# Routed experts computed on tokens sorted by expert, in two groups of batches

## The chip, the cores and the metric

The kernel runs on one core of a Trainium2 chip. Its time is the device time of the whole execution, in microseconds (us). A profiled execution records every instruction of the core's engines: TensorE (PE, with its weight loads as PEld), VectorE (DVE), ScalarE (ACT), GpSimd (POOL) and the issuing queue of SyncE (SP). Its span runs from the first to the last recorded instruction; the execution is a little longer than its span.

## The reference

The input x has 8 batches of 512 tokens with 256 features. A gated cross-attention (16 heads of 64, 512 context rows of 128 features) is added to x, and then a gated mixture of experts: 8 experts, of which each token uses the two with the largest router probability.

```python
x = x + tanh(g_xattn) * xattn(layernorm(x), ctx)      # 16 heads, softmax over 512 rows

xt = layernorm(x)                                     # 4096 tokens x 256
probs = softmax(xt @ gate_w.T)                        # 8 experts
routing_weights, selected = top_k(probs, 2)
comb = sum(one_hot(selected, 8) * routing_weights)    # zero but for two experts a token
for e in range(8):
    out = out + (xt @ expert_w[e].T + expert_b[e]) * comb[:, e:e+1]
x = x + tanh(g_ffn) * out
```

All of it is float32. The reference multiplies every token by every expert and lets the zeros of `comb` remove six of eight.

## The kernel before

A batch is 16 steps (`NS`), and the eight batches follow one another without a gap. A step handles two units; a unit is 128 query tokens of one pair of heads. Each step s does this, in program order:

1. `scores` of its two units on TensorE and `softmax` (the row maximum L230 on DVE, two exponentials L234 on ACT for each unit);
2. side work that is put early: `load_batch` and `experts`;
3. for the units of the step before, the 32x32 transposes on DVE (L255) and, in every even step, `exchange`: 16 transfers of 128 KB between partitions, issued by SP (L266), which finish the transposition of the probabilities; and for its own units the normalisation on POOL (L245);
4. the rest of the side work: projections (`proj_q`, `proj_k`, `proj_v`), attention times values (`values`, three steps after the exchange), `out_proj`, LayerNorm, router and so on.

There is no planner that weighs costs. The list built by `at(b, r, fn)` says in which step (16 b + r) a piece of side work stands, and the list `rank` says in which order the pieces of one step are emitted. Every engine works through its own part of that order and never overtakes. Buffers come from rotating pools (four PSUM banks called `ps_m` for all side work, two of double size, `ps_s`, for the scores).

The expert layer of batch b lies in the steps 22 to 51 after the batch's start, so it runs under the attention of the next two batches. `ln_stats`, `ln_rstd`, `ln_apply` and `ln_T` make the normalised, transposed tokens; `logits` (L318) and `route1` to `route3` give the gate of each token and expert, in `cg`. `weights_T` and `expert_bias` add the bias. Then 16 calls of `experts`, one a step, multiply 128 tokens by two experts each (L403) and DVE adds the two results to the token rows, each scaled by its gate (L410). All eight experts are done for all tokens. Their weights, 2 MB, stay in `we_sb` from the start. After the last expert of a tile SP writes it out (L414).

The last scores are in step 127. The steps after it finish batch 7 and the dense experts that are left.

Of the kernel before, what the change touches and what calls it, by code (L numbers as in the profile page):

```python
# [9 lines left out]
F32 = mybir.dt.float32  # L10
AF = mybir.ActivationFunctionType
ALU = mybir.AluOpType
AX = mybir.AxisListType

P = 128
LN_EPS = 1e-5


@with_exitstack
def kernel(  # L20
# [29 lines left out]
    const = ctx.enter_context(tc.tile_pool(name="const", bufs=1))  # L50
    xpool = ctx.enter_context(tc.tile_pool(name="xpool", bufs=4))
    work = ctx.enter_context(tc.tile_pool(name="work", bufs=2))
    single = ctx.enter_context(tc.tile_pool(name="single", bufs=1))
    qkp = ctx.enter_context(tc.tile_pool(name="qkp", bufs=2))
    vp = ctx.enter_context(tc.tile_pool(name="vp", bufs=2))
    aop = ctx.enter_context(tc.tile_pool(name="aop", bufs=NP_))
    ppool = ctx.enter_context(tc.tile_pool(name="ppool", bufs=4))
    ptp = ctx.enter_context(tc.tile_pool(name="ptp", bufs=2))
    xTp = ctx.enter_context(tc.tile_pool(name="xTp", bufs=2))
    route = ctx.enter_context(tc.tile_pool(name="route", bufs=2))  # L60
    small = ctx.enter_context(tc.tile_pool(name="small", bufs=4))
# [27 lines left out]
    nc.scalar.dma_start(out=gts[:, 1:2], in_=g_ffn.partition_broadcast(P))  # L89
    bo_bc = const.tile([P, D], F32, name="bo_bc")  # L90
    nc.scalar.dma_start(out=bo_bc, in_=bo.partition_broadcast(P))
    wo_sb = const.tile([P, NP_, D], F32, name="wo_sb")
    gw_sb = const.tile([P, KD, E], F32, name="gw_sb")
    we_sb = const.tile([P, KD, E * O], F32, name="we_sb")

# [3 lines left out]
    rev = const.tile([P, NT, E], F32, name="rev")  # L99
    cgs = [const.tile([P, NT, 32], F32, name=f"cg_{i}") for i in range(2)]  # L100

    ident = const.tile([P, P], F32, name="ident")
# [4 lines left out]
    def late_setup():  # L107

        nc.sync.dma_start(out=wo_sb, in_=wo.rearrange("(c p) d -> p c d", p=P))
        nc.sync.dma_start(out=gw_sb, in_=gate_wT.rearrange("(k p) e -> p k e", p=P))  # L110
        nc.sync.dma_start(out=we_sb, in_=expert_wT.rearrange("(k p) f -> p k f", p=P))
        nc.gpsimd.memset(eb2, 0.0)
        for t in range(NT):
            nc.sync.dma_start(out=eb2[32 * t : 32 * t + E, ts(t % 2, O)], in_=expert_b)
        nc.scalar.activation(tg, gts, AF.Tanh)

        nc.gpsimd.tensor_scalar(tgbo, bo_bc, tg[:, 0:1], 1.0, ALU.mult, ALU.mult)

        for e in range(E):
            nc.gpsimd.memset(rev[:, :, e : e + 1], float(E - e))  # L120

        for cg in cgs:
            nc.gpsimd.memset(cg, 0.0)

    def gate_wo(c):
# [21 lines left out]
    def ln_rstd(b, which):  # L147
        mv = lns[which, b][1]
        ve = small.tile([P, NT], F32, tag="ve", name=f"ve_{which}_{b}")
        nc.vector.tensor_scalar_add(ve, mv[:, :, 1], LN_EPS)  # L150
        rstd = small.tile([P, NT], F32, tag="rstd", name=f"rstd_{which}_{b}")
        nc.gpsimd.tensor_tensor(rstd, ve, mhalf, ALU.pow)
        xn = single.tile([P, NT, D], F32, tag="xn", name=f"xn_{which}_{b}")
        lns[which, b] += [rstd, xn]
# [8 lines left out]
    def ln_T(b, which):  # L163
        xn = lns.pop((which, b))[3]
        xT = xTp.tile([P, KD, N], F32, tag=which, name=f"xT_{which}_{b}")
        xTs[which, b] = xT
        for k in range(KD):
            tp = ps_m.tile([P, NT, P], F32, tag="m", name=f"lnT_{which}_{b}_{k}")
            for t in range(NT):
                nc.tensor.transpose(tp[:, t, :], xn[:, t, ts(k, P)], ident)  # L170
            nc.scalar.copy(xT[:, k, :], tp.rearrange("p t n -> p (t n)"))
# [137 lines left out]

    def te(tag, b, w=E):  # L310
        return route.tile([P, NT, w] if w > 1 else [P, NT], F32, tag=tag, name=f"{tag}_{b}")

# [30 lines left out]
    def route2(b):  # L343
        d1, ex, mk1 = rt[b]

        d2 = te("d2", b)
        nc.vector.scalar_tensor_tensor(d2, mk1, -3.0e38, d1, ALU.mult, ALU.add)
        m2 = te("m2", b, 1)
        nc.vector.tensor_reduce(m2, d2, AX.X, ALU.max)
        eq2 = te("eq2", b)  # L350
        nc.vector.tensor_tensor(eq2, d2, bc(m2), ALU.is_equal)
        key2 = te("key2", b)
        nc.vector.tensor_tensor(key2, eq2, rev, ALU.mult)
        km2 = te("km2", b, 1)
        nc.vector.tensor_reduce(km2, key2, AX.X, ALU.max)
        mk2 = te("mk2", b)
        nc.vector.tensor_tensor(mk2, key2, bc(km2), ALU.is_equal)
        mk = te("mk", b)
        nc.vector.tensor_tensor(mk, mk1, mk2, ALU.add)
        rt[b] = (ex, mk)  # L360

    def route3(b):

        ex, mk = rt[b]
        se = te("se", b, 1)
# [8 lines left out]
        )  # L374
        rt[b] = cg

    def weights_T(b):

        pc = ps_m.tile([P, 512], F32, tag="m", name=f"pc_{b}")[:, :P]
        nc.tensor.transpose(pc, rt[b].rearrange("p t e -> p (t e)"), ident)  # L380
        cgT = work.tile([P, P], F32, tag="cgT", name=f"cgT_{b}")
        nc.scalar.copy(cgT, pc)
        xTs["c", b] = cgT

    def expert_bias(b):
# [7 lines left out]
        for h in range(2):  # L393
            nc.vector.tensor_tensor(
                xs[b][:, 2 * h : 2 * h + 2, :], pbs[h], xs[b][:, 2 * h : 2 * h + 2, :], ALU.add
            )

    def experts(b, t, e2):

        xT, acc, cg = xTs["f", b], xs[b][:, t, :], rt[b]  # L400
        pe = ps_m.tile([P, 2, O], F32, tag="m", name=f"pe_{b}_{t}_{e2}")
# [22 lines left out]

    rank = [load_batch, experts, proj_k, proj_q, expert_bias, proj_v, weights_T, out_proj]
    rank += [ln_T, logits, values, ln_stats, ln_rstd, ln_apply, add_bias, gate_wo]
    rank += [route1, route2, route3]

    for b in range(B):
        if b > 0:  # L430
# [4 lines left out]
            for t in range(NT):  # L435
                at(b, -7, ln_apply, b, "q", t)
            at(b, -6, ln_T, b, "q")
            at(b, -5, add_bias, b)
            at(b, -2, proj_q, b, 0)
# [8 lines left out]
        for hp in range(NP_):  # L448
            at(b, 2 * hp + 5, values, b, hp)
        for half in range(2):  # L450
            for t in range(NT):
                at(b, 13 + 8 * half + 2 * t, out_proj, b, half, t)
        for t in range(NT):
            at(b, 22 + 2 * t, ln_stats, b, "f", t)
        at(b, 28, ln_rstd, b, "f")
        for t in range(NT):
            at(b, 29, ln_apply, b, "f", t)
        at(b, 30, ln_T, b, "f")
        at(b, 31, logits, b)
        at(b, 32, route1, b)  # L460
        at(b, 33, route2, b)
        at(b, 34, route3, b)
        at(b, 35, weights_T, b)
        at(b, 36, expert_bias, b)
        for i in range(NT * E // 2):
            at(b, 36 + i, experts, b, i // (E // 2), i % (E // 2))
    for c in range(NP_ // 2):
# [20 lines left out]
    for s in range(max(plan) + 1):  # L488
# [4 lines left out]
        for fn, args in side:  # L493
            if fn in (load_batch, experts):
                fn(*args)
# [8 lines left out]
        for fn, args in side:  # L504
            if fn not in (load_batch, experts):
                fn(*args)
# [37 lines left out]
```

## Time and profile before

| | |
|---|---|
| median of 3 runs | 1126.23 us (1124.82 to 1130.35) |
| the profiled execution | 1126.08 us |
| its span | 1124.2 us |
| TensorE busy | 1098.1 us, 98% of the span |
| VectorE busy | 865.1 us, 77% |
| ScalarE busy | 516.3 us, 46% |
| GpSimd busy | 384.2 us, 34% |
| HBM read and written | 11.71 MB and 4.19 MB |

A page of the profile gives the busy time of each engine, the busy share of 40 slices of the span in tenths, the chain of work that ended last, and the costliest groups of instructions with their mean duration. The trace behind it can be asked for single stretches of time, for the order of an engine's instructions, and for waits. Matrix products appear as two instructions each[...]: the `x8` of a step's scores are four products.

### The profile page before, as it was taken

The numbers are of one execution on the slowest core, as the hardware profiler recorded it, in microseconds if no ns is written. First come the engines' busy times: TensorE is split into PE (matmuls) and PEld (weight loads), VectorE is DVE, ScalarE is ACT, GpSimd is POOL, SyncE is SP. The second block draws the span as 40 slices with busy tenths as digits, with TensorE's granted clock in tenths as the row PEclk, the third lists the DMA queues.
The fourth block names the chain that finished last, engine by engine and source line by source line (L and its number), as shares of the span: only waits on it lengthen the run. The fifth ranks groups of instructions, "written<-read, shape, count | busy, mean of one in ns | idle before, by whom it ended". The sixth has DMA issues, their size and how long they took to land.

```text
span 1124.2 us, 13833 instructions
## 1 busy us (share of the span) xinstructions
PE 1098.1 (98%) x4008; PEld 496.2 (44%) x4008; DVE 865.1 (77%) x1448; ACT 516.3 (46%) x1330; POOL 384.2 (34%) x559
## 2 busy tenths in 40 slices
PE   6889999999999999999999999999999999999898
PEld 3334444544444444444445444444444444445443
DVE  4797788787887878878878778779787787786365
ACT  4666566554544444544444445445445445443000
POOL 4545335433343224323333323432334232331000
PEclk9999999999999999999999999999999999999899
DMA  6877786667555566556565475565665564565100
GB/s 221 191 163 167 172 189 150 150 150 171 122 120 133 127 157 143 113 129 139 138 141 128 107 172 133 113 150 113 146 154 118 118 145 111 129 152 132 35 15 19
DMA packets 61880, 151.05 MB, mean 134 GB/s; under 512 B 17872, under 2 KB 27248, under 8 KB 61552
## 3 DMA queue, kind: packets, MB, share of 16 engines
q1 hardware_dynamic: 60816, 148.75, 57.6%
q10 hardware_dynamic: 992, 1.44, 0.3%
q8 instruction: 33, 0.54, 0.2%
q14 instruction: 39, 0.32, 0.1%
HBM read 11.71 MB, written 4.19 MB: 14 GB/s over the span
## 4 chain that ended last, share of the span: by engine, by line
PE 91%; DVE 3%; SPq 3%; DMA 1%; issue 1%; ACT 0%; ACTq 0%; DVEq 0%
PE pe L403 20%; PE sc L220 20%; PE av L280 19%; PE po L298 10%; PE pq L199 9%; PE pk L209 5%; PE pv L189 5%; SPq L266 3%; PE pl L318 1%; DVE nm L230 1%; DVE tt L255 1%; PE pb L389 1%; PE lnT_f L170 1%; PE lnT_q L170 1%; DMA pt<-tt 0%
## 5 line engine op out<-in xcount | busy, mean ns | idle before, releaser
L245 POOL TENSOR_SCALAR p<-p,rs 128x512 f32<-128x512 f32 x512 | 345.0, 693 | 627.1 <-DVE rs L243 627.1
L234 ACT ACTIVATE p<-sc,nm 128x512 f32<-128x512 f32 x512 | 344.7, 685 | 234.6 <-DVE nm L230 230.4
L230 DVE TENSOR_REDUCE nm<-sc 128x2 f32<-128x1024 f32 x256 | 300.9, 1216 | 155.0 <-PE sc L220 155.0
L255 DVE STREAM_TRANSPOSE tt<-p 128x1024 f32<-128x1024 f32 x256 | 310.4, 1229 | 0.5 <-DMA pt<-tt 0.3
L220 PE MATMUL sc<-k,q 64*128 64x512 f32 x1024 | 256.6, 619 | 7.6 <-ACT p L234 7.6
L403 PE MATMUL pe<-we_sb,xT_f 128*128 128x512 f32 x512 | 246.9, 612 | 0.0
L280 PE MATMUL av<-pt,v 128*64 128x512 f32 x1024 | 236.6, 604 | 4.9 <-DMA out<-x 3.6
L410 DVE SCALAR_TENSOR_TENSOR x<-pe,cg,x 128x256 f32<-128x256 f32 x256 | 123.8, 484 | 75.8 <-PE pe L403 71.0
L403 PEld LDWEIGHTS pe<-we_sb,xT_f 128*128 128x128 f32 x512 | 89.1, 189 | 146.7 <-issue 115.7
L220 PEld LDWEIGHTS sc<-k,q 64*128 64x128 f32 x1024 | 88.3, 187 | 140.7 <-issue 108.3
L286 ACT COPY ao<-av 128x512 f32<-128x512 f32 x64 | 37.5, 586 | 228.9 <-PE av L280 228.9
L280 PEld LDWEIGHTS av<-pt,v 128*64 128x64 f32 x1024 | 68.6, 138 | 137.3 <-issue 128.0
L298 PE MATMUL po<-wo_sb,ao 128*128 128x256 f32 x512 | 122.1, 381 | 0.0
L199 PE MATMUL pq<-xT_q,wq_sb 128*128 128x512 f32 x256 | 121.3, 596 | 0.0
L298 PEld LDWEIGHTS po<-wo_sb,ao 128*128 128x128 f32 x512 | 95.9, 190 | 41.7 <-issue 29.3
L234 ACT ACTIVATION_READ_ACCUMULATOR p<-sc,nm 128x1 f32 x512 | 103.7, 203 | 0.0
L199 PEld LDWEIGHTS pq<-xT_q,wq_sb 128*128 128x128 f32 x256 | 48.9, 192 | 61.5 <-issue 59.3
L209 PE MATMUL pk<-ctxT,wk_sb 128*128 128x512 f32 x128 | 68.3, 615 | 6.8 <-DMA wk_sb<-in_wk 6.8
L189 PE MATMUL pv<-wv_sb,ctxT 128*128 128x256 f32 x256 | 66.2, 381 | 0.0
L189 PEld LDWEIGHTS pv<-wv_sb,ctxT 128*128 128x128 f32 x256 | 48.1, 190 | 35.2 <-issue 18.9
L203 ACT ACTIVATE q<-pq 128x512 f32<-128x512 f32 x64 | 38.8, 606 | 36.3 <-PE pq L199 36.3
L193 ACT COPY v<-pv 128x512 f32<-128x512 f32 x64 | 37.9, 593 | 20.1 <-PE pv L189 20.1
(61 smaller groups left out, 386.4 us busy)
## 6 DMA issues: line engine op xcount, KB each, us to landing
pt<-tt SPq DMA_DIRECT2D x1024, 128.0 KB, 2.4
out<-x SPq DMA_DIRECT2D x32, 128.0 KB, 2.1
x<-in_x SPq DMA_DIRECT2D x7, 512.0 KB, 3.8
ctxT<-in_ctxT SPq DMA_DIRECT2D x8, 256.0 KB, 2.9
we_sb<-in_expert_wT SPq DMA_DIRECT2D x1, 2048.0 KB, 12.8
wo_sb<-in_wo SPq DMA_DIRECT2D x1, 1024.0 KB, 12.5
wk_sb<-in_wk ACTq DMA_DIRECT2D x1, 512.0 KB, 5.5
wq_sb<-in_wq SPq DMA_DIRECT2D x1, 512.0 KB, 7.0
```

What stands on the lines that cost most here:

```text
L189: nc.tensor.matmul(pv[:, r, :], lhsT=cts[b][:, ts(2 * h + r, P)], rhs=wv_sb[:, ts(g, 2 * P)], start=True, stop=True,)
L199: nc.tensor.matmul(pq, lhsT=wq_sb[:, k, ts(hp, P)], rhs=xTs["q", b][:, k, :], start=(k == 0), stop=(k == KD - 1),)
L209: nc.tensor.matmul(pk, lhsT=wk_sb[:, ts(hp, P)], rhs=cts[b], start=True, stop=True)
L220: nc.tensor.matmul(sc[:, j, :], lhsT=q[ts(j, HD), ts(nt, P)], rhs=kt[ts(j, HD), :], start=True, stop=True,)
L230: nc.vector.tensor_reduce(nm, sc, AX.X, ALU.max, negate=True)
L234: nc.scalar.activation(p[:, :, j, :], sc[:, j, :].rearrange("p (q c) -> p q c", q=4), AF.Exp, bias=nm[:, j : j + 1], accum_out=ss[:, j : j ...
L245: nc.gpsimd.tensor_scalar(p[:, :, j, :], p[:, :, j, :], rs[:, j : j + 1], 1.0, ALU.mult, ALU.mult)
L255: nc.vector.transpose(tts[b, hp][:, :, nt, :], p.rearrange("p q j c -> p (q j c)").rearrange("p (k l) -> p k l", l=32),)
L280: nc.tensor.matmul(av[ts(j, HD), :], lhsT=v[:, mt, c : c + HD], rhs=pt[:, :, j, mt, :], start=(mt == 0), stop=(mt == MT - 1),)
L298: nc.tensor.matmul(po, lhsT=aos[b, c][:, ts(t, P)], rhs=wo_sb[:, c, :], start=(i == 0), stop=(i == HC - 1),)
L403: nc.tensor.matmul(pe.rearrange("p a o -> p (a o)"), lhsT=xT[:, k, ts(t, P)], rhs=we_sb[:, k, ts(e2, 2 * O)], start=(k == 0), stop=(k == K ...
L410: nc.vector.scalar_tensor_tensor(acc, pe[:, a, :], cg[:, t, e : e + 1], acc, ALU.mult, ALU.add)
```

## The change

The batches are put into two groups, 0 to 3 and 4 to 6. For a batch of a group the routing is the same, but the dense `experts` calls are gone. In their place:

- `ranks` (TensorE) and `places` (DVE) count, for each of the two chosen experts of a token, its place in that expert's list. `scatter` (POOL, eight indirect DMAs a batch) writes token numbers into eight lists in DRAM, which `clear_lists` has zeroed. `keep_xn` and `keep_x1` (SP) write the normalised tokens and the token rows so far to DRAM.
- After a group's last batch `load_lists` brings the lists back, and `plan1` to `plan4` (DVE, and one small matmul) compute for every tile of 128 list places the expert, the token rows, and for every token where its two results will lie. A group of n batches has 8n + 8 tiles: 40 and 32.
- `fetch` takes two tiles: two indirect DMAs on POOL gather the token rows, and SP reads each tile's expert number into a register and loads that expert's 256 KB of weights from the address in it. Two steps later `sorted_T` transposes the rows, and one step after that `sorted_mm` multiplies them and ACT writes the results to `ysort` in DRAM.
- After all pairs of a group `combine` takes one tile of tokens a step: SP loads the token rows, two indirect DMAs on POOL gather the two results of each token. One step later `combine2` adds them with their weights on DVE, and SP writes the tile out.

Group 0 is planned in steps 80 to 83, fetched in 83 to 102, multiplied in 86 to 105, combined in 107 to 123. Group 1 is planned in steps 128 to 131, fetched in 131 to 146, multiplied in 134 to 149 and combined in 151 to 163. Batch 7 keeps its dense `experts` (steps 149 to 164), with weights that `load_experts` loads in step 131. The resident `we_sb` is gone. Some pools are smaller, and `out_proj` and the LayerNorms stand in other steps. Within a step `sorted_mm` is early, like `experts`; `combine2` stands before `fetch` and `combine`.

```diff
-    xpool = ctx.enter_context(tc.tile_pool(name="xpool", bufs=4))
+    xpool = ctx.enter_context(tc.tile_pool(name="xpool", bufs=3))
-    aop = ctx.enter_context(tc.tile_pool(name="aop", bufs=NP_))
+    aop = ctx.enter_context(tc.tile_pool(name="aop", bufs=NP_ - 2))
-    xTp = ctx.enter_context(tc.tile_pool(name="xTp", bufs=2))
+    xTp = ctx.enter_context(tc.tile_pool(name="xTp", bufs=1))
+    moe = ctx.enter_context(tc.tile_pool(name="moe", bufs=2))
+    wep = ctx.enter_context(tc.tile_pool(name="wep", bufs=2))
+    comb = ctx.enter_context(tc.tile_pool(name="comb", bufs=2))
...
-        nc.sync.dma_start(out=we_sb, in_=expert_wT.rearrange("(k p) f -> p k f", p=P))
...
+    def ranks(b):
+        mk = rt[b][1].rearrange("p t e -> p (t e)")
+        pr = ps_m.tile([P, 512], F32, tag="m", name=f"pr_{b}")[:, : 2 * NT * E]
+        nc.tensor.matmul(pr[:, : NT * E], lhsT=tri, rhs=mk, start=True, stop=True)
+        nc.tensor.matmul(pr[:, NT * E :], lhsT=ones, rhs=mk, start=True, stop=True)
...
+    def places(b):
+        cg, _, mk1, mk2, pr = rt[b]
+        g = group_of[b]
+        pos = te("pos", b)
+        for t in range(NT):
+            nc.vector.tensor_tensor(pos[:, t], pr[:, 0, t], cnt[g], ALU.add)
+            nc.vector.tensor_tensor(cnt[g], pr[:, 1, t], cnt[g], ALU.add)
...
+        for k, mk in enumerate((mk1, mk2)):
+            nc.vector.tensor_copy(mine(mks[g, k], b), mk)
+            pm = te("pm", b)
+            nc.vector.tensor_tensor(pm, mk, pos, ALU.mult)
+            nc.vector.tensor_reduce(mine(addrs[g, k], b), pm, AX.X, ALU.add)
+            nc.vector.tensor_copy(ai[:, k], mine(addrs[g, k], b))
+            wm = te("pm", b)
+            nc.vector.tensor_tensor(wm, mk, cg[:, :, :E], ALU.mult)
+            nc.vector.tensor_reduce(mine(wts[g, k], b), wm, AX.X, ALU.add)
...
+    def scatter(b, t):
+        for k in range(2):
+            nc.gpsimd.indirect_dma_start(
+                out=lists[g, 2 * t + k][:, :],
+                out_offset=bass.IndirectOffsetOnAxis(ap=rt[b][1][:, k, t : t + 1], axis=0),
+                in_=lin[:, c : c + 1], in_offset=None)
...
+    def load_lists(g):
+        li = single.tile([P, 2 * NT, P], I32, tag="xn_f", name=f"li_{g}")
+        for i in range(2 * NT):
+            nc.sync.dma_start(
+                out=li[:, i, :], in_=lists[g, i].rearrange("(j l) o -> j (l o)", l=P))
...
+    def plan3(g):
...
+        nc.vector.tensor_reduce(
+            la, plans.pop((g, "li")).rearrange("p i l -> p l i"), AX.X, ALU.add)
+        pr = ps_m.tile([P, 512], F32, tag="m", name=f"rows_{g}")[:, :T]
+        nc.tensor.matmul(pr, lhsT=la, rhs=sel, start=True, stop=True)
...
+    def fetch(g, i):
+        ei, rows, _ = plans[g]
+        xg = moe.tile([P, 2, D], F32, tag="xg", name=f"xg_{g}_{i}")
+        for a in range(2):
+            T = 2 * i + a
+            nc.gpsimd.indirect_dma_start(
+                out=xg[:, a, :], out_offset=None, in_=xn_d[g][:, :],
+                in_offset=bass.IndirectOffsetOnAxis(ap=rows[:, T : T + 1], axis=0))
+        w = wep.tile([P, 2, KD, O], F32, tag="w", name=f"w_{g}_{i}")
+        for a in range(2):
+            T = 2 * i + a
+            e = nc.sync.value_load(ei[0:1, T : T + 1], min_val=0, max_val=E - 1)
+            nc.sync.dma_start(
+                out=w[:, a].rearrange("p k o -> p (k o)"),
+                in_=expert_wT[bass.ds(e, 1)].rearrange("e p f -> p (e f)"))
...
+    def sorted_T(g, i):
+        tp = ps_m.tile([P, KD, 2, P], F32, tag="m", name=f"xgt_{g}_{i}")
+        for a in range(2):
+            for k in range(KD):
+                nc.tensor.transpose(tp[:, k, a, :], xg[:, a, ts(k, P)], ident)
+        xt = single.tile([P, KD, 2, P], F32, tag="xgT", name=f"xgT_{g}_{i}")
+        nc.scalar.copy(xt, tp)
...
+    def sorted_mm(g, i):
+        py = ps_m.tile([P, 2, O], F32, tag="m", name=f"py_{g}_{i}")
+        for a in range(2):
+            for k in range(KD):
+                nc.tensor.matmul(py[:, a, :], lhsT=xt[:, k, a, :], rhs=w[:, a, k, :],
+                                 start=(k == 0), stop=(k == KD - 1))
+        y = moe.tile([P, 2, O], F32, tag="y", name=f"y_{g}_{i}")
+        nc.scalar.copy(y, py)
+        nc.scalar.dma_start(out=ysort[g][2 * i * P : 2 * (i + 1) * P, :]..., in_=y)
...
+    def combine(b, t):
+        acc = comb.tile([P, D], F32, tag="acc", name=f"acc_{b}_{t}")
+        nc.sync.dma_start(out=acc, in_=x1d[b][:, t, :])
+        for k in range(2):
+            yg = comb.tile([P, D], F32, tag=f"yg{k}", name=f"yg_{b}_{t}_{k}")
+            nc.gpsimd.indirect_dma_start(
+                out=yg, out_offset=None, in_=ysort[g][:, :],
+                in_offset=bass.IndirectOffsetOnAxis(ap=back[k][:, c : c + 1], axis=0))
...
+    def combine2(b, t):
+        for k in range(2):
+            nc.vector.scalar_tensor_tensor(
+                acc, combs.pop((b, t, k)), wts[g, k][:, c : c + 1], acc, ALU.mult, ALU.add)
+        nc.sync.dma_start(out=out[b, ts(t, P), :], in_=acc)
...
-    rank = [load_batch, experts, proj_k, proj_q, expert_bias, proj_v, weights_T, out_proj]
-    rank += [ln_T, logits, values, ln_stats, ln_rstd, ln_apply, add_bias, gate_wo]
-    rank += [route1, route2, route3]
+    rank = [load_batch, sorted_mm, experts, proj_k, proj_q, expert_bias, proj_v, sorted_T]
+    rank += [out_proj, weights_T, ln_T, logits, values, ln_stats, ln_rstd, ln_apply, add_bias]
+    rank += [gate_wo, sort_setup, combine2, route1, route2, route3, ranks, places]
+    rank += [clear_lists, scatter, plan1, plan2, load_lists, plan3, plan4, fetch, combine]
+    rank += [keep_xn, keep_x1, load_experts]
...
+        for t in range(NT):
+            at(b, 13 + t, out_proj, b, 0, t)
+            at(b, 20 + t, out_proj, b, 1, t)
+            at(b, 21 + t, ln_stats, b, "f", t)
+            at(b, 25, ln_apply, b, "f", t)
...
+            at(b, 30, ranks, b)
+            at(b, 31, places, b)
+            for t in range(NT):
+                at(b, 32 + t // 2, scatter, b, t)
...
+    for g, (b0, b1) in enumerate(GROUPS):
+        r = 32
+        at(b1 - 1, r, plan1, g)
+        at(b1 - 1, r + 1, plan2, g)
+        at(b1 - 1, r + 1, load_lists, g)
+        at(b1 - 1, r + 2, plan3, g)
+        at(b1 - 1, r + 3, plan4, g)
+        for i in range(NTILES[g] // 2):
+            at(b1 - 1, r + 3 + i, fetch, g, i)
+            at(b1 - 1, r + 5 + i, sorted_T, g, i)
+            at(b1 - 1, r + 6 + i, sorted_mm, g, i)
+        r += 6 + NTILES[g] // 2 + 1
+        for i, (b, t) in enumerate((b, t) for b in range(b0, b1) for t in range(NT)):
+            at(b1 - 1, r + i, combine, b, t)
+            at(b1 - 1, r + 1 + i, combine2, b, t)
```

## The prediction

> **What bounds the kernel now.** I read the page's busy shares first, then one batch without dense expert work against one with it, then the order of work inside a step, then the issuing queue, then the end. A step below is one pass of the main loop: two units of attention, then the planned side work.
>
> ```profile
> PE 1098.1 (98%) x4008; PEld 496.2 (44%) x4008; DVE 865.1 (77%) x1448; ACT 516.3 (46%) x1330; POOL 384.2 (34%) x559
> ...
> DMA  6877786667555566556565475565665564565100
> ...
> PE 91%; DVE 3%; SPq 3%; DMA 1%; issue 1%; ACT 0%; ACTq 0%; DVEq 0%
> ```
>
> TensorE is busy all the time and is the chain, so removed matmuls pay while nothing else is near. The stretches say how near:
>
> ```profile
> 111.80:219.10 107.30, 107.30 (x436) 49.38 (x434) 87.18 (x131) 62.76 (x164) 47.49 (x68) 1.00 0.76 171
> ...
> 484.70:620.80 136.10, 136.10 (x503) 61.78 (x501) 108.86 (x181) 64.72 (x166) 47.41 (x67) 1.00 0.59 134
> ...
> 1014.90:1124.20 109.30, 100.24 (x311) 48.06 (x310) 58.64 (x144) 7.73 (x20) 6.40 (x9) 0.97 0.21 51
> ```
>
> (Columns: PE, PEld, DVE, ACT, POOL busy, clock, DMA share, GB/s.) Batch 1 (16 steps) has no dense experts and takes 107.3 us; batch 5 has 16 calls and takes 136.1. Without them DVE is already at 81% and the DMA engines at 76%. The third stretch is everything after the last scores begin: 109.3 us, TensorE-bound. Start to start on TensorE's timeline:
>
> ```profile
> 111.79 1.99 PE L220 MATMUL sc<-k,q 64*128 64x512 f32 x8
> ...
> 117.34 1.99 PE L220 MATMUL sc<-k,q 64*128 64x512 f32 x8
> ...
> 124.77 1.99 PE L220 MATMUL sc<-k,q 64*128 64x512 f32 x8
> ...
> 484.75 1.99 PE L220 MATMUL sc<-k,q 64*128 64x512 f32 x8
> 486.66 1.98 PE L403 MATMUL pe<-we_sb,xT_f 128*128 128x512 f32 x4
> ...
> 492.01 1.99 PE L220 MATMUL sc<-k,q 64*128 64x512 f32 x8
> ```
>
> A pair of steps is 5.55 + 7.43 = 13.0 us without experts (13.6 as a mean of a whole batch, LayerNorm and logits included); the same even step with one experts call is 7.26. So a call costs 7.26 - 5.55 = 1.71 us. Last, SP's queue:
>
> ```profile
> 303.32 10.02 SPq L266 DMA_DIRECT2D pt<-tt  x16
> 313.44 0.53 SPq L414 DMA_DIRECT2D out<-x  x1
> ...
> pt<-tt SPq DMA_DIRECT2D x1024, 128.0 KB, 2.4
> out<-x SPq DMA_DIRECT2D x32, 128.0 KB, 2.1
> ```
>
> Every even step's exchange holds SP for 10.1 us (16 issues of 0.59 us, 0.045 between), though each transfer lands after 2.4 us. SP is in order: what stands behind an exchange starts 10 us later. Today only loads that are early and outputs that nobody awaits stand there.
>
> **The change, part by part, up to the start of the last scores (today at 1014.9 us).**
>
> Dense calls removed there: batches 0 to 4 whole and 11 of batch 5, 91 x 1.71 = -155.6 us.
>
> Sorted pairs added there: group 0 has 40 tiles, 20 pairs. A pair is four transposes (the lnT row's eight instructions, 0.86 us) and four 128x256 matmuls (as in one out_proj, 1.73): 2.6 us, 20 x 2.6 = +52. TensorE gains less than top-2 of 8 suggests: each call did two experts at 512 columns, and now there are transposes and one padding tile for each expert. Two ranking matmuls a batch, four instructions of 0.106 (logits: 16 in 1.69): six batches, +2.5.
>
> DVE: places adds 21 small operations a batch; at the routing rows' 0.18 to 0.35 us that is 4.2 us in one step, just after routing, and the f LayerNorm now stands close to it. Adding both engines step by step from step 24 on, DVE lags up to 2.7 us, and the exponentials behind it hold the next scores: I take 3.5 us a batch for batches 0 to 2 (+10.5); later ones lie under longer steps. If DVE kept up it would be 0; if every operation took the 0.52 us of the slow routing rows, 25.
>
> Planning of group 0 (steps 80 to 83): about 9 us of DVE work, and one matmul on TensorE that waits for the lists: four scatters on POOL, landing, eight loads on SP (0.5 each), landing, a 1.2 us reduction. TensorE's queue (the next scores) stands behind it: +14 (5 to 25).
>
> Fetch steps: SP adds two weights a step, each an issue of 0.44 (the 128-row loads at the start), a register load and a little arithmetic. No row shows a register load; [...]I take 0.9. Two steps then need 10.2 + 4 x 1.55 = 16.4 us of SP against 2 x 9.4 of TensorE: hidden, +3 for ACT's output issues. Its cover goes above 2.1 us a load. DMA engines: (4.8 + 2.9)/9.4 a step, 82%, hidden too.
>
> Combine steps (107 to 123) I find the dearest. In SP's order a pair of steps is: exchange, out(i), load acc(i+1), out(i+1), load acc(i+2), next exchange. The acc load stands behind 16 issues, DVE waits for it in combine2, and behind combine2 in DVE's queue stand the next step's two maxima and two transposes, which the next exchange needs. The loop closes: 10.2 exchange + 0.6 out + 2.4 acc from issue to landing + 0.1 + 0.95 combine2 (two at 0.48, the L410 row) + 5.1 (2 x 1.22, 2 x 1.23, reciprocal) = 19.4 us where TensorE needs 13.6. Eight pairs of steps: 8 x 5.8 = +46.
>
> [...]The row says 0.635 us x 16 against 2.4 to land; I take the row.
>
> Sum: 1014.9 - 155.6 + 52 + 2.5 + 10.5 + 14 + 3 + 46 = 987.3 us for the start of the last scores.
>
> **After it (today 109.3 us, 63 of it dense experts that cover all latencies).** All of group 1 runs here, with no attention to hide it. From the last scores, 0:
> - DVE finishes that step with batch 6's places, then the last transposes, at 13; exchange issues to 23; list loads behind it land at 30; reduction, matmul, copy 32; first gather, transposes, first sorted matmul at 38.
> - 16 pairs. transposes -> ACT copy -> matmuls are serial on TensorE, xgT having one buffer: 0.86 + 0.1 + 0.6 + 0.1 + 1.73 = 3.4 a pair; with batch 7's out_proj and logits between, 62: to 100.
> - Output copy, store (2.1 to 2.6), first gathers and combine2: 107.
> - 12 combines. out(i) is ahead of acc(i+1) on SP: 0.6 + 2.4 + 0.1 + 0.95 = 4.1 each, 11 x 4.1 + 1.6 for batch 7's outputs: 154; last expert sums and landing: 158. Batch 7's dense calls (27 us) lie under this.
>
> **Gathers** have no row. POOL's smallest row (the power on 128x4, L152) takes 1.02 us, a 128-row issue on SP 0.44; [...]2.5 my high end. I take 1.2, near the POOL row. At 1.2 POOL does 2.4 a pair, under the 3.4; above 1.7 it sets the pace.
>
> Total: 987.3 + 158 = 1145.3 against the span of 1124.2. The profiled execution took 1126.08 us, 1.9 outside the span, and the median shown is 1126.23; so 1147 us, 1.9% slower. Faster or slower by 0.5% (5.6 us) is about what a measurement can tell here.
>
> **Rivals.**
> - The combine loop does not close (an acc load comes in time, because issues or landings are shorter): 1147 - 46 = 1101 us, faster. For it: DVE has 19% free in batch 1, and SP idles 3 us in each pair today. Against: SP's order and the 10 us rows. It decides below a loop of 16.8 us: there the excess, 8 x 3.2, equals the 21 us forecast as loss. Chance 0.17.
> - Gathers are dear (2.5 us each): pairs take 5, combines 5, scatters and planning 10 more: 26 + 11 + 10, about 1195 us. For it: 184 such DMAs on one in-order engine, 56 of them in the open end. Against: the 1.02 row. 0.15.
> - The end is shorter: the pairs run at TensorE's own 2.6 us and routing does not stall: 13 + 10 less, 1124 us, no change. 0.10.
> - My sum: 0.58.
>
> The main case alone: 1130 to 1165. The range reaches to both outer cases, 1108 to 1195. Faster: the 0.17 and a little of the short end, 0.19; same 0.09; slower 0.72.
>
> **What would show it.** Right: scores 16 steps apart at 108 to 111 us in batches 1 to 4; in steps 108 to 123 pairs of about 19 us, DVE's idle before combine2 ended by the acc load, TensorE's share there near 70%; about 158 us behind the last scores, with combines 4 us apart. Wrong: combine steps at 13.6 a pair; POOL rows of the gathers over 1.7 us; an SP register load over 2 us, which would stretch the fetch steps; the end under 135 us.

## The result and the profile after

The changed kernel takes 1233.98 us (median; 1231.36 to 1239.47) against 1127.2 us for the kernel before on the same chip: 1.095 times as long, 95% interval 1.0905 to 1.0999. The forecast was 1147 us in a range of 1108 to 1195. Slower was right; the size was not: +107 us instead of +21. The profiled execution took 1234.18 us with a span of 1232.4.

First the page of the changed kernel: busy time, the DMA engines' busy share in 40 slices (tenths), and the engines' shares in the chain that ended last.

```profile
PE 1042.6 (85%) x4024; PEld 507.1 (41%) x4024; DVE 818.1 (66%) x1483; ACT 549.6 (45%) x1402; POOL 572.4 (46%) x755
...
DMA  3978867877778768876586788876757666678843
...
PE 40%; DVE 20%; DMA 18%; SPq 11%; ACT 5%; issue 4%; POOL 0%; ACTq 0%; DVEq 0%; POOLq 0%
```

TensorE is busy only 56 us less than before, although by the forecast's own costs (an estimate: 112 calls less, 36 pairs and seven rankings more) its work fell by 95 us. Most of the difference is likely work at a lower clock: with the loops cut, in the run of 1125.58 us below, the same instructions keep it busy 1012.5 us at a mean clock of 0.96 for 0.92. TensorE is no longer the chain: DVE, transfers and SP's issuing now take half of it. The DMA engines, which fell mostly to 5 or 6 tenths before once dense experts ran, now stay mostly at 6 to 8 nearly to the end. The stretches say where. Columns: stretch and its length; busy time of PE, PEld, DVE, ACT and POOL; granted TensorE clock, DMA share, GB/s. They are batch 1, batch 4's sixteen steps, the planning steps, the rest of steps 80 to 106, the steps with combinations (107 to 122), and all after the last scores.

```profile
112.70:221.20 108.50, 107.35 (x441) 50.30 (x439) 92.19 (x155) 63.14 (x166) 47.62 (x68) 1.00 0.76 174
454.90:565.80 110.90, 108.64 (x443) 50.51 (x441) 95.25 (x170) 63.23 (x166) 55.49 (x75) 1.00 0.77 169
565.80:605.00 39.20, 26.43 (x92) 10.81 (x92) 28.49 (x61) 14.58 (x39) 16.71 (x21) 0.83 0.67 143
605.00:858.70 253.70, 218.95 (x875) 119.94 (x871) 139.55 (x248) 114.13 (x281) 117.73 (x148) 0.91 0.77 186
858.70:1029.00 170.30, 124.37 (x445) 55.76 (x443) 108.33 (x191) 63.75 (x168) 86.94 (x105) 0.85 0.65 151
1060.00:1232.40 172.40, 107.04 (x397) 61.67 (x396) 58.48 (x162) 26.13 (x53) 69.07 (x73) 0.84 0.64 180
```

The first two are as forecast: without dense experts sixteen steps take 108 to 111 us and TensorE is full. Batches 2 and 3, for which the forecast named the same range, take 120.2 and 113.5 us. In each of the other stretches shown TensorE has gaps, and the granted clock is lower as well.

To place the miss, the forecast is split at the same steps: each stage of the kernel before, less 1.71 us for each dense call in it, plus the terms that the forecast puts there. (The 91 calls before the last scores are 44, 27, 16 and 4 in the first four rows.)

| stage, us | before | forecast | after | after - forecast |
|---|---|---|---|---|
| start to step 80 | 620.8 | 557.7 | 565.8 | +8.1 |
| steps 80 to 106: plan and fetch | 227.7 | 251.0 | 292.9 | +41.9 |
| steps 107 to 122: combine | 135.2 | 154.3 | 170.2 | +15.9 |
| steps 123 to 126 | 31.1 | 24.3 | 31.0 | +6.7 |
| after the last scores | 109.3 | 158.0 | 172.4 | +14.4 |
| span | 1124.2 | 1145.3 | 1232.4 | +87.1 |

Half of the miss is in steps that the forecast called hidden. There, this is what SP's queue waits for, over the whole run (us in total, times, longest):

```profile
SPq L322 <- DVE rs L299: 163.0, 51, 16.7
SPq L656 <- DVE acc L653: 68.3, 18, 8.1
SPq L322 <- DMA ysort<-y: 42.1, 14, 6.8
SPq L322 <- DMA pt<-tt: 24.9, 21, 3.4
SPq L597 <- PE py L618: 20.9, 14, 7.9
SPq L597 <- DMA ysort<-y: 14.2, 4, 7.1
```

The third and the last line are the odd ones. L322 is the exchange and L597 a weight load. Neither shares data with `ysort<-y`, the store of the experts' results, which ACT issues; yet SP stands 56 us for it. What they share is seen in the semaphore events of the trace. Each transfer in it names a completion semaphore, which its landing raises. SP's 1228 transfers and ACT's 42 name the same eight, mostly in turn, POOL's 184 another eight; and of the 1262 transfers of SP and ACT whose semaphore had served one before, none was issued before that one had landed. A store that ACT issued at 663.73 us landed at 667.70; the next exchange transfer on the same semaphore was issued at 667.71. Seven transfers later the same happens with the store that lands at 675.97 (next transfer at 675.99), and a weight load waits for the store of 701.39. SP's queue shows the holes, seven transfers up to 671.4, then nothing until 675.99, and again nothing from 693.6 to 701.5:

```profile
663.89 12.60 SPq L322 DMA_DIRECT2D pt<-tt  x10
677.32 3.73 SPq L597 DMA_DIRECT2D w<-in_expert_wT  x4
681.16 12.42 SPq L322 DMA_DIRECT2D pt<-tt  x16
701.51 1.45 SPq L597 DMA_DIRECT2D w<-in_expert_wT  x2
```

The late store is late because ACT issues it behind the copy of y, which waits for the matmul, which waits for the weights: a loop from SP through the weights, TensorE and ACT back to SP. On TensorE's timeline (start, duration, and in brackets the idle time before and what ended it) the sorted matmuls stand for weights, and two scores are 12.4 us apart; elsewhere in these steps it is up to 22.6:

```profile
701.19 1.99 PE L276 MATMUL sc<-k,q 64*128 64x512 f32 x8
704.24 1.10 PE L618 MATMUL py<-w,xgT 128*128 128x256 f32 x4 [1.06 <-DMA w<-in_expert_wT]
705.88 1.13 PE L618 MATMUL py<-w,xgT 128*128 128x256 f32 x4 [0.54 <-DMA w<-in_expert_wT]
713.56 1.99 PE L276 MATMUL sc<-k,q 64*128 64x512 f32 x8
```

### The profile page after: what moved, and what is told of

The parts are those of the page before. It is cut to its first block, busy times and chain, and to the rows that moved or that the text cites. A ratio compares the mean times of both kernels' runs of the same rounds, so it can differ in the third digit from the quotient of the medians.

```text
span 1232.4 us, 15004 instructions
## 1 busy us (share of the span) xinstructions
PE 1042.6 (85%) x4024; PEld 507.1 (41%) x4024; DVE 818.1 (66%) x1483; ACT 549.6 (45%) x1402; POOL 572.4 (46%) x755
## 4 chain that ended last, share of the span: by engine, by line
PE 40%; DVE 20%; DMA 18%; SPq 11%; ACT 5%; issue 4%; POOL 0%; ACTq 0%; DVEq 0%; POOLq 0%
PE av L336 10%; PE sc L276 10%; SPq L322 9%; DVE nm L286 7%; DVE tt L311 6%; DMA pt<-tt 6%; DMA acc<-x1d 5%; PE po L354 5%; PE pq L255 4%; ACT p L290 4%; PE py L618 4%; DMA ysort<-y 3%; PE pk L265 3%; DMA w<-in_expert_wT 2%; PE pv L245 2%
## 5 line engine op out<-in xcount | busy, mean ns | idle before, releaser
L301 POOL TENSOR_SCALAR p<-p,rs 128x512 f32<-128x512 f32 x512 | 348.9, 700 | 510.8 <-DVE rs L299 510.4
L276 PE MATMUL sc<-k,q 64*128 64x512 f32 x1024 | 272.7, 651 | 36.3 <-ACT p L290 36.1
L336 PE MATMUL av<-pt,v 128*64 128x512 f32 x1024 | 247.3, 627 | 12.6 <-DMA pt<-tt 12.6
L618 PE MATMUL py<-w,xgT 128*128 128x256 f32 x288 | 80.1, 423 | 44.0 <-DMA w<-in_expert_wT 27.7
L589 POOL DMA_INDIRECT xg<-xn_d,rows x72 | 70.2, 975 | 63.8 <-PE xgt L608 26.1
L653 DVE SCALAR_TENSOR_TENSOR acc<-yg,wt,acc 128x256 f32<-128x256 f32 x56 | 30.5, 545 | 90.7 <-DMA acc<-x1d 83.7
L618 PEld LDWEIGHTS py<-w,xgT 128*128 128x128 f32 x288 | 55.8, 205 | 72.2 <-issue 32.9
L265 PE MATMUL pk<-ctxT,wk_sb 128*128 128x512 f32 x128 | 73.3, 655 | 6.6 <-DMA wk_sb<-in_wk 6.6
L639 POOL DMA_INDIRECT yg<-ysort,back x56 | 55.8, 996 | 45.1 <-DVE acc L653 21.3
L245 PE MATMUL pv<-wv_sb,ctxT 128*128 128x256 f32 x256 | 67.2, 386 | 8.8 <-ACT k L266 8.8
L255 PEld LDWEIGHTS pq<-xT_q,wq_sb 128*128 128x128 f32 x256 | 48.7, 191 | 61.7 <-issue 58.5
L358 DVE TENSOR_TENSOR x<-po,x 128x256 f32<-128x256 f32 x64 | 26.3, 411 | 71.3 <-PE po L354 71.3
```

The source lines that it names most:

```text
L245: nc.tensor.matmul(pv[:, r, :], lhsT=cts[b][:, ts(2 * h + r, P)], rhs=wv_sb[:, ts(g, 2 * P)], start=True, stop=True,)
L255: nc.tensor.matmul(pq, lhsT=wq_sb[:, k, ts(hp, P)], rhs=xTs["q", b][:, k, :], start=(k == 0), stop=(k == KD - 1),)
L265: nc.tensor.matmul(pk, lhsT=wk_sb[:, ts(hp, P)], rhs=cts[b], start=True, stop=True)
L276: nc.tensor.matmul(sc[:, j, :], lhsT=q[ts(j, HD), ts(nt, P)], rhs=kt[ts(j, HD), :], start=True, stop=True,)
L301: nc.gpsimd.tensor_scalar(p[:, :, j, :], p[:, :, j, :], rs[:, j : j + 1], 1.0, ALU.mult, ALU.mult)
L336: nc.tensor.matmul(av[ts(j, HD), :], lhsT=v[:, mt, c : c + HD], rhs=pt[:, :, j, mt, :], start=(mt == 0), stop=(mt == MT - 1),)
```

## The experiments

They go from the fetch steps to the first scatters, the combination, the planning and the end. Stage times are read between the starts of the scores, as in the table, each in one profiled execution. The runs with smaller weights, without scatters and with filler are a single execution; executions of one kernel here lie up to 16.5 us apart (order swapped alone: 1203.55 to 1220.03), so their stages say more than their times.

**Stores on another queue.** The store leaves ACT; it stands behind the normalisations of the same step on POOL, whose transfers (184 in the changed kernel) have eight completion semaphores of their own.

```diff
         nc.scalar.copy(y, py)
-        nc.scalar.dma_start(
+        ys[g, i] = y
...
+    def store_y(g, i):
+        y = ys.pop((g, i))
+        nc.gpsimd.dma_start(
             out=ysort[g][2 * i * P : 2 * (i + 1) * P, :].rearrange("(a p) o -> p a o", p=P), in_=y
         )
```

> The stores of the experts' results leave ScalarE's queue: VectorE's neighbour GpSimd issues each one behind the normalisations of the same step. Theory A (a transfer of SP whose completion semaphore is shared with one of those stores has to wait until it has landed): the waits of the exchange and of the weight loads for a store, 56 us in the trace of the changed kernel, go, the 26 steps from 80 to 106 take 265 to 275 us where they took 293, and the kernel takes 1205 to 1218 us where it took 1234. Theory B (the transfers themselves back up, the weights above all): the waits go but the weights land as late as before, and the time stays between 1225 and 1240 us.

Measured: 1197.01 us (ratio to before 1.0607, 1.056 to 1.0654), 37 us less. Steps 80 to 106 take 250.5 us, the forecast's 251, with the full weights. No wait for a store is left on SP:

```profile
SPq L322 <- DVE rs L299: 168.9, 49, 16.4
SPq L662 <- DVE acc L659: 66.0, 18, 7.1
SPq L322 <- DMA pt<-tt: 28.9, 23, 7.5
```

The DMA share of these steps went up from 0.76 to 0.88, so the transfers were not the limit before (behind the planning steps it is 0.93 now, with little room left). Theory A has the cause, and the gain of 42 us in these steps is larger than it expected. Part of that is the clock: with the gaps gone it rose from 0.90 to 0.97, and TensorE's busy time for the same instructions fell from 245.4 to 230.3 us. The move also takes the store off ACT's queue; a store left on ACT with semaphores of its own, which would part the two, was not run. The end became 7 us longer (179.6): a pair takes 4.17 us there for 3.79, with three transfers issued by POOL.

**Smaller weights.**

```diff
-        w = wep.tile([P, 2, KD, O], F32, tag="w", name=f"w_{g}_{i}")
+        w = wep.tile([P, 2, 128], F32, tag="w", name=f"w_{g}_{i}")
...
-                out=w[:, a].rearrange("p k o -> p (k o)"),
-                in_=expert_wT[bass.ds(e, 1)].rearrange("e p f -> p (e f)"),
+                out=w[:, a], in_=expert_wT[bass.ds(e, 1)].rearrange("e p f -> p (e f)")[:, :128],
...
-                    py[:, a, :], lhsT=xt[:, k, a, :], rhs=w[:, a, k, :],
+                    py[:, a, :], lhsT=xt[:, k, a, :], rhs=w[:, a].unsqueeze(1).to_broadcast([P, O // 128, 128]),
```

> The changed kernel, but every weight load moves 64 KB instead of 256 KB and the matmuls read these columns over and over (three quarters of the experts' weights are left out); registers, issues, buffers and waits stay. Theory A (a shared completion semaphore behind ScalarE's store): the steps from 80 to 106 take 270 us or more where they took 293, and SP still waits 30 us or more for stores. Theory B (the bytes of the weights back the transfers up): 255 us or less.

Measured: 1214.88 us; steps 80 to 106 take 271.1 us. SP still waits 39 us for stores (22.7 with an exchange behind them, 16.6 with a weight load). That is theory A's side, at its edge. Bytes matter (22 us), probably as a part of the loop, since weights that land earlier make the store earlier. With the loop cut, the full weights cost nothing beyond the forecast.

An earlier form of this run held the weights in two fixed buffers:

```diff
-        w = wep.tile([P, 2, KD, O], F32, tag="w", name=f"w_{g}_{i}")
+        w = wtiles[i % 2]
```

> Each weight load keeps its register, its issue and its waits but moves 32 KB instead of 256 KB, into buffers that are otherwise zero (most of the experts' weights are left out). Theory A (shared semaphores): the 26 steps from 80 to 106 lose less than 10 of their 293 us. Theory B (the bytes back up): they fall by 25 us or more, the exchange lands in about 2.5 us again, and the time is 1200 us or less.

Measured: 1302.74 us, 354.8 us in those steps. It says nothing on the two theories: `fetch` of pair i+2 stands before the matmuls of pair i in program order, so with fixed buffers a pair waits for the weights meant for two pairs later. A rotating pool gives each pair its own tile and has no such wait.

**Stores later on ACT.** The same function as in the first run, issued by ACT behind its copies of that step.

```diff
     def store_y(g, i):
         y = ys.pop((g, i))
-        nc.gpsimd.dma_start(
+        nc.scalar.dma_start(
```

> The changed kernel, with the stores of the experts' results still on ScalarE but at the end of the same step, behind the copies of the next pair and of the projections. Theory A (SP waits for the landing of a store that shares its semaphore): a later store is waited for longer, SP's waits for stores rise from 56 us to 65 us or more, and the kernel takes 1237 to 1265 us. If it is ScalarE's own work behind the store that is held up, the move frees it and the time falls to 1225 us or less.

Measured: 1231.54 us (1.0944, 1.0913 to 1.0975), SP's waits for stores 61 us. Neither expectation holds. In group 0 a store now leaves 3.1 us behind its copy on average, up to 7.3, where it left after 0.03; SP's waits rise by 5 us only, and why a later store costs no more stays open. That ACT's copies no longer stand behind the store is worth about 2 us here (1231.54 for 1233.98), so it doesn't explain the 37 us of the first run.

**No scatters.** The lists are left empty.

```diff
-                at(b, 32 + t // 2, scatter, b, t)
+                pass
```

> The changed kernel without the scatters of the lists, so that every list stays zero and all sorted places hold the first row of the group. If the first scatters delay the exchange of step 35, that step takes 5.5 us instead of 15.0 and step 80 begins at 552 to 558 us instead of 565.8; if the stall there has another cause, the step stays at 13 us or more.

Measured: 1212.3 us; step 80 begins at 552.8 us instead of 565.8, and the stall is gone. TensorE's timeline from step 34 on, the changed kernel first, then without scatters:

```profile
236.20 1.99 PE L276 MATMUL sc<-k,q 64*128 64x512 f32 x8
241.76 1.99 PE L276 MATMUL sc<-k,q 64*128 64x512 f32 x8
256.73 1.99 PE L276 MATMUL sc<-k,q 64*128 64x512 f32 x8
```

```profile
235.55 1.99 PE L276 MATMUL sc<-k,q 64*128 64x512 f32 x8
241.10 1.99 PE L276 MATMUL sc<-k,q 64*128 64x512 f32 x8
246.60 1.99 PE L276 MATMUL sc<-k,q 64*128 64x512 f32 x8
```

15.0 us become 5.5. On SP the exchange of that time takes 12.96 us with scatters under way and 10.02 without, and in the changed kernel its first four transfers land after 2.3 to 2.4 us, eleven of the other twelve after 7.5 us and more (one after 5.5). How the scatters hold them up inside the DMA engines isn't shown, and why the first batch suffers most (9.5 us of the 13) isn't settled. Batches 2 and 3 take 110.7 and 110.8 us now.

**The kept rows on POOL.** Now the combination.

```diff
-        nc.sync.dma_start(out=acc, in_=x1d[b][:, t, :])
+        nc.gpsimd.dma_start(out=acc, in_=x1d[b][:, t, :])
```

> The load of the kept rows for the combination is issued by GpSimd ahead of its two gathers instead of by SP. Theory A (the loop in which SP's exchange, the kept rows, the combination and the store of the result wait for each other sets the pace): the sixteen steps with a combination, 170 us, take 120 to 130 us, and the tail's combinations come every 4 us or less instead of every 4.7; the kernel takes 1170 to 1190 us. Theory B (the gathers' own landing or GpSimd sets the pace, and the kept rows are only the last of several to arrive): the wait moves from the kept rows to the gathered ones, and the time stays within 15 us of 1234.

Measured: 1207.55 us (1.0712, 1.0695 to 1.073); the sixteen steps take 149.8 us, not 120 to 130, and the 84 us that DVE stood for kept rows are gone. In their place DVE stands 47.9 us for the gathered rows, as theory B had it, but the time fell by more than B allows. It is half of the gain that A expected: POOL now waits for the buffers (`POOL acc L636 <- DMA out<-acc`, 30.8 us), since a load reuses the buffer of two combinations before and that one must have been written out.

**Both moves.** The two diffs above together.

> Both moves of the two runs before it. If the two losses lie in different stages, the gains add up: if theory A holds for both, 1145 to 1172 us, still slower than the kernel before the change (1127). If GpSimd, which then issues four software transfers per pair of steps beside the normalisations, becomes the limit, the time is above the better of the two.

Measured: 1167.41 us (1.0367, 1.035 to 1.0385). The gains add up: 37 + 26 = 63 us singly and 67 us together, so the two losses are separate.

**Four buffers.** On the kernel with both moves.

```diff
-        acc = comb.tile([P, D], F32, tag="acc", name=f"acc_{b}_{t}")
+        acc = comb.tile([P, D], F32, tag="acc", bufs=4, name=f"acc_{b}_{t}")
```

> The kernel with both moves (1167 us) with four buffers for the kept rows instead of two. Theory (a load of kept rows waits until the result of two combinations before has landed, so two combinations take 8.3 us at the end): the twelve combinations of the tail come every 3.0 to 3.4 us instead of every 4.2, the sixteen steps with combinations take 128 to 138 us instead of 145, and the kernel takes 1140 to 1155 us. Rival (the gathers' landing sets the pace): within 5 us of 1167.

Measured: 1142.94 us (1.0154, 1.0137 to 1.0171). The sixteen steps take 136.2 us, and the tail's loads of kept rows come every 3.46 us (1103.53 to 1141.57 us, twelve of them), a little over the expected 3.4. POOL's queue says why not less:

```profile
1118.45 0.59 POOL L642 DMA_DIRECT2D acc<-x1d  x1
1119.34 1.11 POOL L645 DMA_INDIRECT yg<-ysort,back  x1 [0.30 <-DMA yg<-ysort,back]
1120.76 0.98 POOL L645 DMA_INDIRECT yg<-ysort,back  x1 [0.31 <-issue]
1121.74 0.59 POOL L642 DMA_DIRECT2D acc<-x1d  x1
```

It does nothing but issue: 3.3 us for three transfers. (This profiled execution took 1152.8 us, the longest of this kernel; its stages may be a little long.)

**Filler on TensorE.** On the changed kernel: does the lower clock cost time, or only follow from the gaps?

```diff
+    def filler(s):
+        f = ps_m.tile([P, 512], F32, tag="m", name=f"fill_{s}")
+        for k in range(2):
+            nc.tensor.matmul(f, lhsT=ident, rhs=wk_sb[:, :512], start=True, stop=True)
...
+        if 107 <= s < 123:
+            filler(s)
```

> The changed kernel with two matmuls of 128x512 added at the end of each of the sixteen steps 107 to 122, 27 us of TensorE's time at full clock. If the lower granted clock there (0.85) only follows from TensorE's gaps and the gaps set the time, the clock rises above 0.9 and the sixteen steps stay at 167 to 174 us. If the lower clock itself costs time, they fall to 160 us or less. If TensorE has no time to spare there, they rise to 185 us or more.

Measured: 1231.75 us. The sixteen steps, and the four behind them:

```profile
859.50:1029.60 170.10, 148.59 (x509) 65.55 (x507) 110.18 (x191) 64.46 (x169) 89.42 (x108) 0.93 0.67 155
1029.60:1056.30 26.70, 25.84 (x117) 12.71 (x116) 21.48 (x37) 12.64 (x35) 8.32 (x13) 1.00 0.74 179
```

24 us more of TensorE's work cost nothing and raised the clock from 0.85 to 0.93: in these steps the low clock follows from the gaps. The second line was not expected. Without filler these four steps took 31.0 us at a clock of 0.81, TensorE busy throughout; here they take 26.7 at 1.00. The clock that the gaps lowered was paid for in the full stretch behind them, 4.3 us here. TensorE's timeline of the changed kernel shows it, at the border of the two stretches:

```profile
1027.94 1.11 PE L226 MATMUL lnT_f<-ident,xn_f 128*128 128x128 f32 x4 [8.76 <-ACT k L266]
1028.99 3.79 PE L276 MATMUL sc<-k,q 64*128 64x512 f32 x8
...
1041.95 1.99 PE L276 MATMUL sc<-k,q 64*128 64x512 f32 x8
```

Behind a gap of 8.76 us the same eight matmuls take 3.79 us instead of 1.99; the granted clock is 0.50 from 1025 to 1038 us, 0.68 in the next 4 us, and 1.00 from 1042 us on. So it stays at 0.50 for 12.6 us of full work. Behind the gaps before 250.84 (7.1 us) and before 943.44 us (10.4 us) that is only 4.7 and 5.0 us, and what makes the difference isn't shown. The forecast had no term for the long gaps that its own loops opened: in the stretches it saw, the clock was at 1.00, and at 0.97 behind the last scores.

**Later plan.** On the kernel with four buffers, `plan3` and all behind it two steps later, so that the lists have landed.

```diff
+        r += 2
         at(b1 - 1, r + 2, plan3, g)
```

> The kernel with both moves and four buffers (1143 us), in which the third and fourth plan step and all that follows of a group come two steps later. If the 18 us of step 82 are VectorE's wait for the lists, which the scatters of the last batch hold back, the steps 80 to 84 take 36 to 40 us instead of 48, and the kernel takes 1131 to 1139 us. If the wait only moves to the later step, 1141 to 1146 us.

Measured: 1139.99 us (1.0124, 1.0104 to 1.0144). Steps 80 to 84 fall from 48.4 to 39.9 us as expected, but the medians are only 3 us apart, with intervals that overlap. The two profiled executions are 8.2 us apart, and each is the longest of its kernel, so how much of the 8.5 us reaches the time isn't settled.

**The tail's queues.** On that kernel, and for group 1 alone, the stores go back to ACT and the kept rows to SP.

```diff
-        nc.gpsimd.dma_start(
+        eng = nc.gpsimd if g == 0 else nc.scalar
+        eng.dma_start(
...
-        nc.gpsimd.dma_start(out=acc, in_=x1d[b][:, t, :])
+        (nc.gpsimd if g == 0 else nc.sync).dma_start(out=acc, in_=x1d[b][:, t, :])
```

> The kernel with the later plan, but for the second group, which runs when no exchange is left, ScalarE issues the stores of the results again and SP the loads of the kept rows, so that GpSimd has two gathers per pair or combination instead of three transfers. If GpSimd's issue sets the pace of the tail (3.3 us per combination), combinations come every 2.4 to 2.8 us and pairs every 3.2 us or less, and the kernel takes 8 to 15 us less than the one with the later plan alone. If the gathers' landing sets it, within 3 us of that one.

Measured: 1147.63 us (1.0195, 1.017 to 1.0219), 8 us more, which neither side expected. Pairs are quicker (3.84 us for 4.16), but combinations take 4.7 us again, with four buffers:

```profile
1094.12 0.34 SPq L663 DMA_DIRECT2D out<-acc  x1
1094.51 0.42 SPq L643 DMA_DIRECT2D acc<-x1d  x1
1098.81 0.34 SPq L663 DMA_DIRECT2D out<-acc  x1
1099.20 0.42 SPq L643 DMA_DIRECT2D acc<-x1d  x1
```

SP issues the store of a result, which waits for DVE, and only then the rows for the next one. The loop would then be SP's order, which the next run tests.

**Order swapped.** `combine2` behind `combine`, in that kernel and in the changed kernel alone.

```diff
-    rank += [gate_wo, sort_setup, combine2, route1, route2, route3, ranks, places]
-    rank += [clear_lists, scatter, plan1, plan2, load_lists, plan3, plan4, fetch, combine]
+    rank += [gate_wo, sort_setup, route1, route2, route3, ranks, places]
+    rank += [clear_lists, scatter, plan1, plan2, load_lists, plan3, plan4, fetch, combine, combine2]
```

> The version with SP's loads in the tail (1148 us), in which a step's load of kept rows is issued before the store of the result before it, no longer behind it. If the order on SP is what made its combinations 4.7 us, they come every 2.4 to 3.1 us in the tail and the kernel takes 1120 to 1132 us, no longer clearly slower than the kernel before (1126). If the gathers' landing sets it, 1143 us or more.

> The changed kernel with that order swapped and nothing else (two buffers, all on SP). If the order on SP sets the loop, the sixteen steps with combinations take 148 to 158 us instead of 170, the tail's combinations come every 3.4 us instead of 4.7, and the kernel takes 1198 to 1214 us. If the two buffers set it by themselves, the sixteen steps stay above 165 us and the time above 1225 us.

In the changed kernel alone: 1212.03 us (1.0757, 1.0706 to 1.0808), as forecast for the order; but the sixteen steps fall only to 161.6 us, between the two expectations, since with two buffers SP now waits 47 us for results to be written out. The tail's combinations come every 3.1 us. Order and buffers both hold the loop.

In the other: 1125.58 us, 0.9992 of before (0.9971 to 1.0013), so no difference from it can be measured. Its tail, SP's queue:

```profile
1091.35 0.33 SPq L663 DMA_DIRECT2D out<-acc  x1
1091.78 0.38 SPq L643 DMA_DIRECT2D acc<-x1d  x1
1094.16 0.33 SPq L663 DMA_DIRECT2D out<-acc  x1
1094.54 0.42 SPq L643 DMA_DIRECT2D acc<-x1d  x1
```

2.8 us a combination over all twelve. Its stages against the kernel before: start to step 80, 565.7 for 620.8; steps 80 to 106, 239.8 for 227.7; 107 to 122, 132.2 for 135.2; 123 to 126, 28.3 for 31.1; the end, 154.0 for 109.3. So all of the loss against the kernel before goes when transfers are queued, ordered and buffered otherwise and the plan stands later. What then keeps the sorted experts from winning is the end: 45 us more, nearly all that the rest gains.

## Why the prediction was right and wrong

**What TensorE gains: right.** Batches 1 and 4 take 108 to 111 us as forecast, batches 2 and 3 only without scatters; with the store's loop cut steps 80 to 106 take 250.5 us for 251.0. Both fit 1.71 a call and 2.6 a pair.

**"Fetch steps ... hidden, +3": the step that failed.** It cost about 44 us instead of 3: the stage is 41.9 over its forecast, which held the 3, and planning took 0.9 of that. Each cover was counted and was there: SP's work per weight load is even smaller than assumed (issues 1.1 us apart at 677 us, for 1.55; the register load, for which the forecast assumed 0.9 without a row to show it, takes 0.27, the median of 72 at L596), and the DMA engines had room (a share of 0.77). What was missing is a coupling that no count of work shows: ACT's store, set down as "+3 for ACT's output issues", stands on the same eight completion semaphores as SP's exchange, and SP waited 56 us on them. Whom a late store would hold up was never asked, because nothing waits for its data until the combination.

**The combine loop: right in its mechanism, too small.** This line, the combination on DVE and what ended its idle time, is the one that the forecast named:

```profile
L653 DVE SCALAR_TENSOR_TENSOR acc<-yg,wt,acc 128x256 f32<-128x256 f32 x56 | 30.5, 545 | 90.7 <-DMA acc<-x1d 83.7 <-issue 5.9
```

A pair of steps takes 21.3 us (170.2 for eight) where the forecast had 19.4. The exchange, taken at 10.1 us, holds SP for 12.9 here (16 transfers from 917.34 us), the rows land after up to 4.1 us (one after 7.9) instead of 2.4, and each of a combination's two operations takes 0.545 us for 0.48. One transfer of the exchange took 0.59 us to issue in the kernel before against 2.4 to land, but the rows' load stands behind sixteen in a row. Moving that 128 KB load and giving it four buffers took 34 of the 170 us back. The rival that the loop doesn't close falls with it.

**Gathers: the rival of dear gathers falls.** They take 0.98 and 1.0 us of POOL (L589, L639). The 1.2 of the forecast and the 2.5 of the rival were the author's assumptions. The POOL row of 1.02 us that the 1.2 leans on was not the smallest (L245 takes 0.69 in the kernel before), but the gathers came out near it.

**Scatters and planning.** Planning was forecast at +14 and took 14.9: steps 80 to 83 take 41.0 us, where the kernel before, without its four calls, has 26.1. Step 82 alone is 18 us for 7, and the later plan shows that 8.5 us of the stage were its wait for the lists. What failed is that the scatters were counted as POOL's time only: through step 80 they cost 13 us. DVE's lag was taken too high: without scatters step 80 begins at 552.8 us, 5.6 more than the forecast has without its 10.5 for that lag (547.2). These 4.9 us too many hide a part of the scatters' 13, by luck.

**The end: mechanism right, sizes short.** 172.4 us for 158. Most of the 14 us is lost before the first pair, to the scatters again. Batch 6's are under way while the last exchange is issued, and its transfers land after up to 13.2 us. SP's queue there, the changed kernel first, then without scatters:

```profile
1074.01 18.13 SPq L322 DMA_DIRECT2D pt<-tt  x16
```

```profile
1049.18 10.04 SPq L322 DMA_DIRECT2D pt<-tt  x16
```

The list loads stand behind it. The first gather is issued 41.2 us after the last scores instead of 32, and without scatters at 32.2; the first sorted matmul starts at 50.6 us instead of 38. (Without scatters the whole end is no shorter, 174.5 us, but there every gather reads one row and a pair takes 4.45 us.) The sixteen pairs then take 58.5 us where the forecast had 62 with batch 7's work between them, and combinations 4.6 for 4.1. The rival of a shorter end falls. The combinations follow the order on SP that the forecast wrote out; from its issue the row load took 4.4 us to the next store (1178.71 to 1183.11) instead of 3.4:

```profile
1178.32 0.34 SPq L656 DMA_DIRECT2D out<-acc  x1
1178.71 0.42 SPq L636 DMA_DIRECT2D acc<-x1d  x1
1183.11 0.33 SPq L656 DMA_DIRECT2D out<-acc  x1
1183.53 0.38 SPq L636 DMA_DIRECT2D acc<-x1d  x1
```

**Steps 123 to 126** were to be full and cheap; they were full, but at a mean clock of 0.81; the filler run gives 4.3 of the 6.7 us back.

## What to carry to other kernels

When work moves to another queue, count not only its issues and bytes: ask which queues take their completion semaphores from the same set, and how late the slowest transfer among them can land, because an exchange that has nothing to do with it may wait for it, as it did here for 56 us in all. In an in-order queue write the load for the next round ahead of the store of the last one and give it more than two buffers; here these, other queues for one store and one load, and a later plan went together with 108 us less. Work that is moved behind the last stage that could hide it is paid in full: 45 us of the gain went there.

## What the runs showed of the hardware

- In the changed kernel SP's 1228 and ACT's 42 transfers drew on one set of eight completion semaphores, POOL's 184 on another eight; SP stood 56 us for ACT's stores, and 0 when POOL issued them.
- Scatters of 128 words of 4 bytes take 1.0 us of POOL but land only after 8.3 us (median), and of the sixteen transfers of an exchange issued meanwhile eleven landed after 7.5 us and more, where the kernel before has 2.4 (median). Leaving them out gave 13 us up to step 80 and brought the first gather of group 1 9 us closer to the last scores.
- Behind a gap of 8.8 us the granted TensorE clock stayed at 0.50 for 12.6 us of full work, behind gaps of 7.1 and 10.4 us for 4.7 and 5.0 us; 24 us of filler in the gaps cost nothing and made the full stretch behind them 4.3 us shorter (one execution each).
